# Two classes of edges in a graph network: rows of one class by one-hot products, of the other by gathers

## The chip, the cores and the metric

The kernel runs on one core of a Trainium2 chip. A core has five engines with a queue of instructions each: TensorE (PE, matrix products into PSUM; "PEld" are its weight loads), VectorE (DVE), ScalarE (ACT), GpSimd (POOL) and SyncE (SP). An engine takes its instructions in order and waits at the first whose semaphores are not reached. Transfers are issued from the queues of SP, ACT and POOL. The metric is the device time of one execution in microseconds. The PE clock that the throttle grants is told as a share of full speed.

## The reference

There are 3125 nodes with 128 features, and 53,125 edges: 25,000 random pairs in both directions and a self loop for each node, sorted by destination. Four networks follow each other, each added to its input and layer-normalised:

```python
x = LN(x + gin(x))       # 4 layers: h = x + sum of x[src] per dst; x = relu(h@W1+b1)@W2+b2
x = LN(x + relu(x@root + bias + sum_r mean over edges of type r of (x[src] @ W[r])))     # 8 types
x = LN(x + relu(sum over edges of alpha[type]*(x@w_rel[type])[src] + count*(x@update)))  # 16 types, 8 bases
x = LN(x + relu(sum over edges of gate*(x[src]@W[r] + bias[r]) + x@loop))                # 8 types
```

## The kernel before

**Dense part.** `gin_layers` (L515) builds the adjacency as a dense bf16 matrix AT of 25 blocks of 128 sources by 3125 destinations. The edges come in TE = 416 tiles of 128. For each tile, DVE writes two one-hots (L824, L826), PE multiplies them (L828, L832), and ACT copies the result into AT at a column held in a register (L835). Besides, `late(i)` (L631) does a piece of other work at the tiles of `LATE = [16, 20, 24, 28, 32, 36]`: it turns the tables of keys and source indices and writes them to DRAM (`keys`, `srcs`). After that `first_parts` splits x into three bf16 parts whose sum is the f32 value. `dense(l, j, …)` (L752) multiplies AT by the parts: 75 bf16 products per chunk of 512 destinations (L760), then the copy hT (L765) and two dense products (L768, L775); seven chunks, four layers. The first of the dense layers runs beside the loop over tiles. `checks` tests on chip that the sorted edges lie near where an even spread would put them and writes a flag; only if the flag is set does a slower program, `any_order`, run after this one.

**Relational part.** `in_order` (L924) loads the keys back, computes registers' values, and runs `relational` (L1092) three times. The edges are processed in the same 416 tiles:

- a gather (L1062): an indirect transfer, issued by POOL, of the 128 source rows into a buffer `xg` of four tiles; there are six such buffers, so gathers may run 24 tiles ahead;
- a one-hot `oh` on DVE (L1150, L1152 or L1157, by layer) of 128 edges by 16 columns x 8 types: since edges are sorted by destination, a tile is taken to touch at most W = 16 destinations;
- an f32 product `pw` on PE (L1159; the profile counts two matmuls for one f32 product), and its addition on DVE into `sums` at a column from a register (L1161). DVE loads 16 such registers at a time (`DGRP`);
- in layers 1 and 3 a product that counts the edges per type, into PSUM at an offset that PE loads to a register (L1167; one or two per tile, 728 in all per layer);
- in layer 2 coefficients per 8 tiles (L1097); in layer 3 gates from gathered columns (L1139, L1141).

When the last tile of a block of 128 destinations is done, `finish1`, `finish2` or `finish3` (L1193, L1260, L1282) multiplies the block's sums by the weights (L1183), normalises and writes the rows to the DRAM table of the next layer (`xtab`, `gtab`, or the output). ACT sets the sums back to zero (`clear`, L956). The next layer's gathers read the whole table, so they wait for the last block.

The order on each engine's queue is fixed when the kernel is built: the framework places instructions by their order in the program and adds semaphores for every dependence, buffers' reuse included.

Of the kernel before, what the change touches and what calls it, by code (L numbers as in the profile page):

```python
# [61 lines left out]
LATE = [16, 20, 24, 28, 32, 36]  # L62
# [452 lines left out]
def gin_layers(ctx: ExitStack, tc: tile.TileContext, a: dict, pre: dict, outer: ExitStack, eps, srcI, xtab):  # L515
# [13 lines left out]
    keys = dram.tile([P, 4, TE], F32, name="keys")  # L529
    srcs = dram.tile([P, TE], I32, name="srcs")  # L530

    AT = big.tile([P, NB, N + W], BF16, name="AT")
    places = keep_.tile([P, 2, TE], F32, name="places")
# [5 lines left out]
    lo, hi = pre["lo"], pre["hi"]  # L539
# [6 lines left out]
    for n, (name, pad) in enumerate((("dst", PADDST), ("src", 0), ("edge_type_8", 0), ("edge_type_16", 0))):  # L546
        eng = (nc.sync, nc.scalar)[n % 2]
        r = raw[name] = tmp.tile([QR, 4, P], I32, name="raw_" + name)
        nc.gpsimd.memset(r[96:QR], pad)
        e = a[name]  # L550
        flat = r.rearrange("q k p -> q (k p)")

        for q0, q1 in ((0, 96), (96, QR - 1)):
            eng.dma_start(flat[q0:q1, :], e[q0 * 4 * P:q1 * 4 * P].rearrange("(q p) -> q p", q=q1 - q0))
        eng.dma_start(flat[QR - 1:QR, :E - (QR - 1) * 4 * P], e[(QR - 1) * 4 * P:].rearrange("(q p) -> q p", q=1))
    early = keep_.tile([P, 1], F32, name="early")
    nc.scalar.copy(early, eps)
    make_identity(nc, ident)
    nc.gpsimd.iota(iotah, pattern=[[1, NK]], base=0, channel_multiplier=0, allow_small_or_imprecise_dtypes=True)
    nc.gpsimd.iota(iota, pattern=[[1, 2 * P]], base=0, channel_multiplier=0, allow_small_or_imprecise_dtypes=True)  # L560
# [11 lines left out]
    def fl(name, into=None):  # L572
        f[name] = into if into is not None else tmp.tile([QR, 4, P], F32, name="f_" + name)
        nc.vector.tensor_copy(f[name], raw[name])
        return f[name]
# [12 lines left out]
    sbI = tmp.tile([QR, 4, P], I32, name="sbI")  # L588
    nc.vector.tensor_scalar(sbI, raw["src"], 7, None, op0=OP.arith_shift_right)
    sb = tmp.tile([QR, 4, P], F32, name="sb")  # L590
    nc.vector.tensor_copy(sb, sbI)
    kb = tmp.tile([QR, 4, P], F32, name="kb")
    nc.vector.scalar_tensor_tensor(kb, sb, float(WK), rel, op0=OP.mult, op1=OP.add)
    mod = tmp.tile([QR, 4, P], F32, name="mod")
# [17 lines left out]
    nc.scalar.copy(hi, dst0[:, 1, :])  # L612
# [11 lines left out]
    def later(i, r):  # L624
        t = tmp.tile([P, TE], F32, name="turned", bufs=2)
        turn(t, r, nc.scalar.copy)
        nc.sync.dma_start(keys[:, i, :], t)

    turnedI = tmp.tile([P, TE], I32, name="turnedI")

    def late(i):  # L631

        if i == 0:
            turn(turnedI, f["src"], nc.vector.tensor_copy)
            nc.sync.dma_start(srcs[:, :], turnedI)
        elif i == 1:
            later(0, rel)
        elif i == 2:
            t8 = fl("edge_type_8", sb)
            later(3, t8)  # L640
        elif i == 3:
            nc.vector.scalar_tensor_tensor(mod, rel, float(R8), f["edge_type_8"], op0=OP.mult, op1=OP.add)
            later(1, mod)
        elif i == 4:
            later(2, fl("edge_type_16", kb))
        elif i == 5:
            flat = f["dst"].rearrange("q k p -> q (k p)")
            inner = f["src"].rearrange("q k p -> q (k p)")[:, :4 * P - 1]
            nc.vector.tensor_tensor(inner, flat[:, :4 * P - 1], flat[:, 1:], OP.is_gt)
            nc.vector.tensor_reduce(found, inner, AX.X, OP.add)  # L650
            tmp_ctx.close()

    def checks(own):
# [25 lines left out]
        add(1, w[:, 0:1], float(N - W), OP.is_lt)  # L679
        rows = own.tile([1, 1], F32, name="rows")  # L680
# [122 lines left out]
    with tc.tile_pool(name="g_hot", bufs=4) as hots:  # L803
        old = None
        under = []
        for t in range(TE):
# [6 lines left out]
            if t == LATE[-1]:  # L813
# [5 lines left out]
                nc.scalar.dma_start(srcI, srcs[:, :])  # L819
                sp_pool = sp_ctx.enter_context(tc.tile_pool(name="g_parts", bufs=1, side="right"))  # L820
            if t % 4 == 1 and (t - LATE[-1]) // 4 - 1 in range(NCH):
                first_parts((t - LATE[-1]) // 4 - 1)
# [22 lines left out]
    keep_ctx.close()  # L845
    ep = outer.enter_context(tc.tile_pool(name="f_edges", bufs=1))
    edges = ep.tile([P, 4, TE], F32, name="edges")
    nc.scalar.dma_start(edges, keys[:, :, :])
# [38 lines left out]
    for j in range(NCH):  # L887
        run(dense(l, j, norm))
    sp_ctx.close()
# [16 lines left out]

def low(t):
# [10 lines left out]
def first_tile(c0):  # L918

    return min(t for t in range(TE) if low(t)[1] + W > c0)  # L920
# [3 lines left out]
def in_order(ctx: ExitStack, tc: tile.TileContext, a: dict, out: bass.AP, pre: dict):  # L924
# [7 lines left out]
    ident, iota, ones, lo = (pre[k] for k in ("ident", "iota", "ones", "lo"))  # L932
# [7 lines left out]
    srcI = own.tile([P, TE], I32, name="f_srcI")  # L940
    edges = gin_layers(tc, a, pre, ctx, eps, srcI, xtab[0])
    dlr, key8, et16, et8 = (edges[:, i, :] for i in range(4))

    big = ctx.enter_context(tc.tile_pool(name="f_sums", bufs=1, side="right"))
    gat = ctx.enter_context(tc.tile_pool(name="f_gat", bufs=6, side="right"))
    ohp = ctx.enter_context(tc.tile_pool(name="f_ohp", bufs=6, side="right"))
# [6 lines left out]
    zero = const.tile([P, 1], F32, name="f_zero")  # L953
    nc.vector.memset(zero, 0.0)

    def clear(b, engine=nc.scalar.copy):  # L956
        engine(sums[:, b * P * NR:(b + 1) * P * NR], zero.to_broadcast([P, P * NR]))  # L957

    clear(0, nc.vector.tensor_copy)


    offs = const.tile([1, TE], I32, name="f_offs")
    nc.vector.tensor_scalar(offs, lo, float(NR), None, op0=OP.mult)
    seg = const.tile([1, 2, TE], I32, name="f_seg")

    def segments(t):
        c = low(t)
        return range(c[0] // SEGN, min(NSEG - 1, (c[1] + W - 1) // SEGN) + 1)

    def spots(t, i):  # L970

        if len(segments(t)) <= i:
            return 0, SEGN + W
        return tuple(min(SEGN + W, max(0, x + W - segments(t)[i] * SEGN)) for x in low(t))

    raw = const.tile([1, TE], F32, name="f_raw")
    nc.vector.memset(raw, 0.0)
    for i in range(2):
        for j in range(NSEG):
            ts = [t for t in range(TE) if len(segments(t)) > i and segments(t)[i] == j]  # L980
            if ts:
                nc.vector.tensor_scalar(raw[:, ts[0]:ts[-1] + 1], lo[:, ts[0]:ts[-1] + 1], float(W - j * SEGN), 0.0,
                                        op0=OP.add, op1=OP.max)
        nc.vector.tensor_scalar(seg[:, i, :], raw, float(SEGN + W), None, op0=OP.min)
# [10 lines left out]
    rW = load("rW", [P, R8, D], a["L1_gnn_W"].rearrange("r i o -> i r o"))  # L995
    root = load("root", [P, D], a["L1_gnn_root"])
    rbias = load("rbias", [1, D], a["L1_gnn_bias"].rearrange("(a o) -> a o", a=1))
    sel = const.tile([R8, R8, P], F32, name="f_sel")
    cnt = const.tile([R8, NP], F32, name="f_cnt")
    zeroh = const.tile([1, SEGN + 2 * W], BF16, name="f_zeroh")  # L1000
# [3 lines left out]
    def later_weights():  # L1004
# [9 lines left out]
        W2["bases"] = load("bases", [P, NBASE, D], a["L2_gnn_weight"].rearrange("b i o -> i b o"))  # L1014
        W2["gW"] = gW = load("gW", [P, R8, D], a["L3_gnn_W"].rearrange("r i o -> i r o"))
# [14 lines left out]
        V = W2["V"] = const.tile([P, R8], F32, name="f_V")  # L1030
        gconst = W2["gconst"] = const.tile([P, R8], F32, name="f_gconst")
        for r in range(R8):
            gg = wk.tile([P, D], F32, name="gg")
            nc.sync.dma_start(gg, row(a["L3_gnn_gate_weight"][r], D))
            gb = wk.tile([P, D], F32, name="gb")
            nc.sync.dma_start(gb, row(a["L3_gnn_bias_term"][r], D))
            nc.vector.tensor_tensor(gb, gb, gg, OP.mult)
            nc.vector.tensor_reduce(gconst[:, r:r + 1], gb, AX.X, OP.add)
            nc.vector.tensor_tensor(gg, gW[:, r, :], gg, OP.mult)
            nc.vector.tensor_reduce(V[:, r:r + 1], gg, AX.X, OP.add)  # L1040
        nc.vector.tensor_add(gconst, gconst, W2["ggb"])

# [8 lines left out]
        dcol = W2["dcol"] = const.tile([P, W, NBASE], F32, name="f_dcol")  # L1051
        nc.vector.tensor_copy(dcol, iota[:, :W].unsqueeze(2).to_broadcast([P, W, NBASE]))

    def values(rowap, engine, bounds):
# [3 lines left out]
            skip_runtime_bounds_check_because="the drift of every tile was checked before this path was taken")  # L1058
# [6 lines left out]
    def hots(keys_, n, name, t):  # L1065

        m = min(GRP, TE - t)
        oh = wk.tile([P, GRP, n], F32, name=name)
        nc.vector.tensor_tensor(oh[:, :m], iota[:, :n].unsqueeze(1).to_broadcast([P, m, n]),
                                keys_[:, t:t + m].unsqueeze(2).to_broadcast([P, m, n]), OP.is_equal)  # L1070
        return oh

    def rows_of(table, b):

        t = wk.tile([P, D], F32, name="xb", bufs=4)
# [16 lines left out]
    def relational(layer, table, width, finish, beside=lambda t: None):  # L1092
        counted = layer in (1, 3)
        segs, cgroups = {}, {}
        b = 0

        def coefficients(t):  # L1097

            m = min(GRP, TE - t)
            oh = hots(et16, R16, "h16", t)  # L1100
# [7 lines left out]
            c = wk.tile([P, GRP, NBASE], F32, name="coef", bufs=3)  # L1108
            nc.scalar.copy(c, pc[:, :GRP * NBASE].rearrange("p (q b) -> p q b", b=NBASE))  # L1109
            cgroups[t] = c  # L1110

        for t in range(TE):
            beside(t)
            if t % DGRP == 0:
                n = min(DGRP, TE - t)
# [227 lines left out]
```

## Time and profile before

| what | value |
|---|---|
| median of 15 runs | 2806.79 us (2798.15 to 2819.14) |
| the profiled execution | 2806.24 us |
| its span | 2804.4 us |
| mean granted PE clock | 0.697 |
| adjacency loop | about 14 to 326 us |
| dense layers 1 to 3 | 344 to 690 us |
| relational layers 1, 2, 3 | 704–1433, 1433–2081, 2081–2804 us |
| gathers: 1248 | 0.95 us of POOL each |

The profile gives for each engine its busy time, its share of the span and the number of its instructions. The span in 40 slices shows each engine's busy tenths. Register loads, branches, semaphores and the issuing of transfers are not counted as busy. A group of instructions is a line, an engine, an operation and its tiles, with the count, the busy time, the mean of one in ns, and behind the second bar the idle time of the engine just before them with what ended it: another engine's instruction, a transfer, "issue" (nothing that the profile shows) or "remote" (an unknown queue). The waits' lines give the engine, the line that waited, for what, and the total, the times and the longest in us.

### The profile page before, as it was taken

The numbers are of one execution on the slowest core, as the hardware profiler recorded it, in microseconds if no ns is written. First come the engines' busy times: TensorE is split into PE (matmuls) and PEld (weight loads), VectorE is DVE, ScalarE is ACT, GpSimd is POOL, SyncE is SP. The second block draws the span as 40 slices with busy tenths as digits, with TensorE's granted clock in tenths as the row PEclk, the third lists the DMA queues.
The fourth block names the chain that finished last, engine by engine and source line by source line (L and its number), as shares of the span: only waits on it lengthen the run. The fifth ranks groups of instructions, "written<-read, shape, count | busy, mean of one in ns | idle before, by whom it ended". The sixth has DMA issues, their size and how long they took to land.

```text
span 2804.4 us, 37365 instructions
## 1 busy us (share of the span) xinstructions
PE 1941.8 (69%) x10916; PEld 1374.2 (49%) x10916; DVE 1162.9 (41%) x4732; ACT 498.0 (18%) x1001; POOL 1195.8 (43%) x1263
## 2 busy tenths in 40 slices
PE   5798999998477667777655665556644656565666
PEld 2343444444355556656544554445533545454555
DVE  6777612123144444444433444344423334343343
ACT  5778501101200000000011222222220000000000
POOL 0000000000555555656546666666635555555552
PEclk9988899999555656565555666666665566566556
DMA  1000112021111111112111122112211221222221
GB/s 49 17 7 13 54 34 61 17 62 51 48 48 43 44 45 43 47 43 52 46 33 49 50 51 52 50 49 53 50 29 44 48 48 45 46 48 46 48 47 28
DMA packets 101231, 121.96 MB, mean 43 GB/s; under 512 B 25045, under 2 KB 80522, under 8 KB 101030
## 3 DMA queue, kind: packets, MB, share of 16 engines
q0 software_dynamic: 40000, 83.59, 12.4%
q1 hardware_dynamic: 50256, 28.48, 3.4%
q10 hardware_dynamic: 10774, 7.42, 0.9%
q8 instruction: 100, 1.64, 0.3%
q14 instruction: 101, 0.83, 0.1%
HBM read 104.55 MB, written 14.84 MB: 43 GB/s over the span
## 4 chain that ended last, share of the span: by engine, by line
PE 46%; another core or an unknown queue 20%; issue 14%; POOL 7%; DVE 7%; DMA 3%; ACT 2%; DVEq 0%; ACTq 0%; SPq 0%; POOLq 0%
PE acc L760 13%; PE pw L1159 12%; POOL xg L1062 7%; PE pm L1183 7%; PE pa L828 3%; PE pr L1204 3%; PE pc L1167 2%; DVE sums L1161 2%; PE pr L768 1%; PE pr L775 1%; DMA xg<-fx,f_srcI 1%; DMA xn<-in_x_dram 1%; PE pa L832 1%; DVE sc L1205 1%
## 5 line engine op out<-in xcount | busy, mean ns | idle before, releaser
L1062 POOL DMA_INDIRECT xg<-fx,f_srcI x832 | 795.0, 956 | 1199.9 <-DMA f_gloop<-n_L_gnn_loop_weight_dram 699.4
L1159 PE MATMUL pw<-oh,xg 128*128 128x128 f32 x2496 | 667.4, 407 | 360.8 <-issue 150.4
L1159 PEld LDWEIGHTS pw<-oh,xg 128*128 128x128 f32 x2496 | 523.2, 282 | 448.3 <-issue 189.9
L1161 DVE TENSOR_TENSOR sums<-pw,sums 128x128 f32 x1248 | 358.2, 287 | 868.9 <-remote 429.8
L1062 POOL DMA_INDIRECT xg<-gtab,f_srcI x416 | 395.3, 950 | 332.9 <-PE pw L1159 170.6
L760 PE MATMUL acc<-AT,xs 128*128 128x512 bf16 (+1 forms) x2100 | 442.4, 355 | 1.2 <-DMA xs<-xsd 1.1
L760 PEld LDWEIGHTS <-xs 128*128 128x128 bf16 x2100 | 175.8, 99 | 195.6 <-issue 20.0
L835 ACT CAST AT<-pa 128x400 f32 x416 | 213.3, 513 | 62.7 <-PE pa L832 27.7
L828 PE MATMUL pa<-ohk,ohs 128*128 128x425 bf16 x416 | 171.4, 426 | 48.6 <-ACT AT L835 25.5
L826 DVE TENSOR_SCALAR ohk<-iotah,places 128x425 bf16<-128x425 f16 x416 | 139.1, 334 | 59.7 <-PE pa L832 53.2
L957 ACT COPY sums<-f_zero 128x1024 f32<-128x1024 f32 x74 | 75.2, 1042 | 367.2 <-PE pm L1183 123.6
L1152 DVE SCALAR_TENSOR_TENSOR oh<-f_dcol,edges,coef 128x128 f32<-128x128 f32 x416 | 136.8, 343 | 0.6 <-ACT coef L1109 0.6
L1157 DVE TENSOR_SCALAR oh<-p_iota,edges,g 128x128 f32<-128x128 f32 x416 | 135.3, 353 | 0.1
L1167 PE MATMUL pc<-hw,h 128*8 128x16 f32 x1456 | 85.8, 186 | 55.8 <-issue 50.8
L1150 DVE TENSOR_SCALAR oh<-p_iota,edges 128x128 f32<-128x128 f32 x416 | 119.7, 295 | 0.0
L1204 PE MATMUL pr<-ci,f_sel 8*128 8x128 f32 x400 | 93.8, 381 | 36.4 <-DVE sc L1205 33.0
L1183 PE MATMUL pm<-f_gW,sums 128*128 128x128 f32 x400 | 100.1, 432 | 24.8 <-DVE sums L1161 18.5
L1167 PE MATMUL pc<-hw,rg 128*8 128x16 f32 x1456 | 84.0, 183 | 39.6 <-issue 20.7
L1183 PEld LDWEIGHTS pm<-f_gW,sums 128*128 128x128 f32 x400 | 97.8, 336 | 26.2 <-DVE sums L1161 19.2
L1183 PE MATMUL pm<-f_bases,sums 128*128 128x128 f32 x400 | 100.4, 434 | 9.0 <-DVE sums L1161 6.0
L1167 PEld LDWEIGHTS pc<-hw,h 128*8 128x8 f32 x1456 | 61.2, 90 | 92.4 <-issue 80.0
L828 PEld LDWEIGHTS <-ohs 128*128 128x128 bf16 x416 | 42.3, 102 | 130.4 <-DVE ohk L826 86.7
(202 smaller groups left out, 1782.9 us busy)
## 6 DMA issues: line engine op xcount, KB each, us to landing
xg<-fx,f_srcI POOLq DMA_INDIRECT x832
xsd<-sp SPq DMA_DIRECT2D x18, 384.0 KB
xg<-gtab,f_srcI POOLq DMA_INDIRECT x416
xs<-xsd SPq DMA_DIRECT2D x9, 384.0 KB
xs<-xsd ACTq DMA_DIRECT2D x9, 384.0 KB
xb<-fx SPq DMA_DIRECT2D x49, 64.0 KB
gtab<-yg SPq DMA_DIRECT2D x25, 68.0 KB
fx<-y SPq DMA_DIRECT2D x25, 64.0 KB
```

The source lines that it names most:

```text
L760: nc.tensor.matmul(acc[:, :n], xs[s // BPB][:, s % BPB, i, :], AT[:, s, c0:c1], start=s == 0 and i == 0, stop=s == NB - 1 and i == 2)
L826: nc.vector.tensor_scalar(ohk, iotah, keyb[:, t:t + 1], None, op0=OP.is_equal)
L828: nc.tensor.matmul(ps, ohs, ohk, start=True, stop=t == 0)
L835: nc.scalar.copy(AT[:, :, bass.ds(og[t % GRP], W)], ps3[:, :, :W])
L1062: nc.gpsimd.indirect_dma_start(out=dst, out_offset=None, in_=table, in_offset=bass.IndirectOffsetOnAxis(ap=idx, axis=0))
L1152: nc.vector.scalar_tensor_tensor(oh.rearrange("p (d b) -> p d b", b=NR), W2["dcol"], dlr[:, u:u + 1], cgroups[u - u % GRP][:, u % GRP, :]. ...
L1157: nc.vector.tensor_scalar(oh, iota[:, :W * NR], key8[:, u:u + 1], gate, op0=OP.is_equal, op1=OP.mult)
L1159: nc.tensor.matmul(ps, x[:, u % 4, :D], oh, start=True, stop=True)
L1161: nc.vector.tensor_tensor(w, ps, w, OP.add)
L1167: nc.tensor.matmul(segs[j][:, bass.ds(spot[i][u], W)], r, hw[:, u % GRP, :], start=False, stop=u == last_tile(min(N, (j + 1) * P)))
L1183: nc.tensor.matmul(pb, s[:, r, :], w[:, r, :], start=False, stop=r == NR - 1)
L1204: nc.tensor.matmul(pr[:, r * P:(r + 1) * P], sel[:, h + r, :], ci, start=True, stop=True)
```

## The change

The source blocks are divided. An edge whose source lies in the last KB = 6 blocks (node S0 = 2432 or above) belongs to class P, every other edge to class G. Both classes keep the order of destinations and are padded to whole tiles: NTP = 96 tiles of P with a window of WP = 48 destinations, NTG = 327 tiles of G with the window of 16.

*Sorting.* `late` no longer turns tables. It computes on DVE, over 125 partitions x 425 edges, each edge's rank in its class by a scan, and from it a slot. 425 `scatter`s, indirect transfers on POOL of 125 entries of 8 bytes (source and destination in one number, types in the other), write the entries to a DRAM table `slots`: one after each tile of the adjacency loop from tile 29 on, the last 38 after it. `first_parts` comes every 8 tiles in place of 4. After the third chunk of the last dense layer `arrange()` reads the slots back, unpacks them on DVE, and writes P's source rows to DRAM as f16.

*Relational layers.* A G tile goes as before, from a table cut to [:S0]. A P tile has no gather: `fetch` makes its 128 rows by products of one-hots of the sources with the six blocks, held in SBUF as three bf16 parts; `add_P` makes the wide product with the one-hot of destinations, adds the one column that an earlier tile may have begun, and copies the result over `sums`, which need no clearing. `upto` puts P tiles ahead of the G tiles that touch the same columns, and fetches one tile more with each G tile. `finish` of the last six blocks splits the new rows for the next layer (`keep_parts`).

Layer 1's counts are multiplied in bf16. Registers are loaded 8 at a time. The buffers for gathers are five, those for one-hots four, and the three 8-weight tables share two buffers; `gate_weights` comes before layer 2, and the checks of the new bounds, `later_keys`, at tile 100 of layer 1.

```diff
+KB = 6
+S0 = (NB - KB) * P
+NTP = 96
+NTG = 327
...
+            nc.vector.tensor_scalar(flag2, raw2["src"], float(S0), None, op0=OP.is_ge)
+            nc.vector.tensor_tensor_scan(rank, flag2, none, 0.0, OP.add, OP.add)
...
+    def scatter(c):
+        st = nc.gpsimd.indirect_dma_start(
+            out=slots[:, :], out_offset=bass.IndirectOffsetOnAxis(ap=rowI[:, c:c + 1], axis=0),
+            in_=meta[:EP2, c, :], in_offset=None)
...
+            if t > LATE[-1]:
+                scatter(t - LATE[-1] - 1)
...
+    def arrange():
+        held = meta[:, :NTT, :]
+        nc.gpsimd.dma_start(held.rearrange("p t f -> p (t f)"), slots.rearrange("(p t) f -> p (t f)", p=P))
+        nc.vector.tensor_copy(edges["dst"], held[:, :, 0])
...
     for j in range(NCH):
         run(dense(l, j, norm))
+        if j == 2:
+            arrange()
...
+    def split(x, to, tmp):
+        nc.scalar.copy(to(0), x)
+        nc.vector.tensor_tensor(tmp, x, to(0), OP.subtract)
+        nc.scalar.copy(to(1), tmp)
+        nc.vector.tensor_tensor(tmp, tmp, to(1), OP.subtract)
+        nc.vector.tensor_copy(to(2), tmp)
...
+        def fetch(v):
+            if v % 2 == 0:
+                srcb = wk.tile([P, 2 * P], F16, name="srcb", bufs=4)
+                nc.sync.dma_start(srcb, flatrow[:, v * P:(v + 2) * P].to_broadcast([P, 2 * P]))
+                ohT = hot_src[0] = wk.tile([P, KB, 2 * P], BF16, name="ohTP")
+                for k in range(KB):
+                    nc.vector.tensor_scalar(ohT[:, k, :], srcb, colid[:, k:k + 1], None, op0=OP.is_equal)
+            if v % 4 == 0:
+                fetched[v // 4] = (wk.tile([P, 4, GX], F32, name="xP"),)
+            ohT, x = hot_src[0], fetched[v // 4][0]
+            px = psum.tile([P, GX], F32, name="px", bufs=1)
+            for k in range(KB):
+                for i in range(3):
+                    nc.tensor.matmul(px[:, :width_], ohT[:, k, v % 2 * P:(v % 2 + 1) * P], parts[layer][:, k, i, :width_],
+                                     start=k == 0 and i == 0, stop=k == KB - 1 and i == 2)
+            nc.scalar.copy(x[:, v % 4, :width_], px[:, :width_])
+
+        def add_P(v):
+            x = fetched[v // 4][0]
...
+            oh = onehot(v, gate)
+            ps = psum.tile([P, BANK], F32, name="pp", bufs=1)
+            nc.tensor.matmul(ps[:, :WP * NR], x[:, v % 4, :D], oh, start=True, stop=True)
...
+            if v > 0:
+                nc.vector.tensor_tensor(ps[:, :NR], ps[:, :NR], sums3[:, bass.ds(g["lo"][q], 1), :].rearrange("p d r -> p (d r)"), OP.add)
...
+            nc.scalar.copy(sums3[:, bass.ds(g["loA"][q], WP), :], ps[:, :WP * NR].rearrange("p (d r) -> p d r", r=NR))
...
+        def upto(need, ahead):
+
+            while done[0] < min(NTP, need // 4 * 4 + 4):
+                fetch(done[0])
+                done[0] += 1
+            while done[1] <= min(need, NTP - 1):
+                add_P(done[1])
+                done[1] += 1
+            if ahead and done[0] < min(NTP, need // 4 * 4 + 8):
+                fetch(done[0])
+                done[0] += 1
...
-    relational(2, xtab[1][:, :], D, finish2)
+        keep_parts(3, b, yg[:, 0, :], GX)
+
+    new_parts(3)
+    gate_weights()
+    relational(2, xtab[1][:S0, :], D, finish2)
...
-    relational(3, gtab[:, :], GX, finish3)
+    relational(3, gtab[:S0, :], GX, finish3)
```

## The prediction

> **What bounds the kernel now.** First the page: shares of the engines, the slices, the chain.
>
> ```profile
> span 2804.4 us, 37365 instructions
> PE 1941.8 (69%) x10916; PEld 1374.2 (49%) x10916; DVE 1162.9 (41%) x4732; ACT 498.0 (18%) x1001; POOL 1195.8 (43%) x1263
> ...
> PE   5798999998477667777655665556644656565666
> ...
> POOL 0000000000555555656546666666635555555552
> PEclk9988899999555656565555666666665566566556
> ...
> PE 46%; another core or an unknown queue 20%; issue 14%; POOL 7%; DVE 7%; DMA 3%; ACT 2%; DVEq 0%; ACTq 0%; SPq 0%; POOLq 0%
> ```
>
> PE is the busiest engine, but only the first quarter (adjacency and dense layers) is dense. In the relational three quarters PE is half to two thirds busy at a granted clock of 0.5 to 0.6, and POOL, idle before, issues gathers. So the stages, by windows: 100–300 lies in the adjacency loop, 344–690 is dense layers 1 to 3, then relational layers 1, 2, 3.
>
> ```profile
> 100.00:300.00 200.00, 184.80 (x980) 81.50 (x979) 153.25 (x628) 156.98 (x307) 0.00 (x0) 0.86 0.03 9
> 344.00:690.00 346.00, 343.23 (x1826) 162.55 (x1825) 69.83 (x167) 34.61 (x60) 0.00 (x0) 1.00 0.15 45
> 704.00:1433.00 729.00, 506.42 (x3222) 412.50 (x3222) 308.01 (x1195) 57.78 (x115) 397.93 (x417) 0.60 0.17 44
> 1433.00:2081.00 648.00, 380.25 (x1605) 317.74 (x1605) 253.33 (x1063) 137.60 (x281) 398.81 (x419) 0.64 0.19 48
> 2081.00:2804.00 723.00, 429.03 (x2830) 359.61 (x2830) 274.89 (x1265) 20.73 (x74) 395.06 (x416) 0.60 0.20 45
> ```
>
> The columns are the window, its length, busy PE, PE weight loads, DVE, ACT, POOL, the clock, DMA share, GB/s. The relational layers take 2100 us: PE busy 1316, idle 784. Does the gather set the pace? Its rhythm when nothing holds it is 0.95 busy and 0.30 of issue, 1.25 us, so 416 tiles need 520 us; the layers take 729, 648 and 723. The POOL's waits in layer 1 (then layer 2), and gathers against sums (L1161) in the first part of layer 1:
>
> ```profile
> POOL xg L1062 <- PE pw L1159: 134.5, 34, 10.3
> ...
> POOL xg L1062 <- PE pw L1159: 35.7, 22, 2.6
> ...
> 703.00:1147.00 444.00, 244.69 (x256) 0.59 0.17 45
> ...
> 703.00:1147.00 444.00, 66.57 (x233) 0.59 0.17 45
> ```
>
> POOL waits 134.5 us in layer 1 for PE to free a gather buffer, and after 444 us it is 256−233 = 23 tiles ahead of 24 possible. So in layers 1 and 3 the consumers (one-hot on DVE, product on PE, sum on DVE, counts on PE) set the pace; in layer 2 the two are near level.
>
> ```profile
> L1159 PE MATMUL pw<-oh,xg 128*128 128x128 f32 x2496 | 667.4, 407 | 360.8 <-issue 150.4
> L1161 DVE TENSOR_TENSOR sums<-pw,sums 128x128 f32 x1248 | 358.2, 287 | 868.9 <-remote 429.8
> L1167 PE MATMUL pc<-hw,h 128*8 128x16 f32 x1456 | 85.8, 186 | 55.8 <-issue 50.8
> ```
>
> PE's gaps end on nothing the profile shows ("issue", "remote"): DVE, PE and ACT stand still together for 3 to 14 us while gathers go on; five-microsecond DVE stops recur about each 16 tiles, where 16 register values are loaded. The change keeps one such load per tile (416 becomes 423).
>
> **Cost, part by part.**
> *A gathered tile dropped.* PE: 667.4/1248 = 0.535 us of product, and in layers 1 and 3 (85.8+84.0)/832 = 0.204 of counts. 89 fewer tiles (416−327).
> *A one-hot tile added, 96 per layer.* Its fetch is 18 bf16 matmuls of 128 columns. The dense layers stream 512 columns in 219 ns, so 128 in 55 ns: 18 × 55 = 0.99 us at full clock. Each also has a new 128x128 weight load (99 ns in the L760 rows), so 18 × 0.10 = 1.8 if loads aren't hidden. I take 1.5, since relational PE shows loads beside matmuls at a low clock. The wide product, 384 f32 columns: three times the 128-column one is 1.5 at the relational clock; the 512-column L768 at full clock takes 1.1 for two passes, so 0.85 for 384. I take 1.2, and 0.1 for counts: 2.8 us (1.9 to 3.4), 269 us a layer (182 to 326). Less what the 89 tiles gave back (66 in layers 1 and 3, 48 in layer 2), and less 33 for layer 1's counts in one bf16 pass instead of two (327×0.204/2): +170, +221, +203, together +594. PE goes from 1316 to 1910 us at today's clock.
> *Clock.* 0.60 at 69% busy, 0.86 at 92%, 1.00 at 99%: at three quarters busy, about 0.70. 1910×0.61/0.70 = 1664.
> [...]
> *Idle.* 784 us over 1248 tiles is 0.63 a tile; 981 tiles keep 617. Fetches (96×3×1.5×0.87 = 376) depend on no gather and can fill it, but PE takes its queue in order and one fetch is issued per gathered tile: half, −188. New handoffs (product, first-column add on DVE, ACT copy into sums, which the next add reads, through one psum buffer): nearest row the bound between pw and sums, about 0.3 us exposed per tile, +86. Idle 515. Relational: 1664+515 = 2179, **+79**. Nothing filled: +267; all filled: −109.
> *DVE.* Per one-hot tile: six one-hots of 256 columns per two tiles (0.284 each, between L824's 0.247 for 128 columns and L826's 0.334 for 425) 0.85; a 384-column one-hot about 0.5 (L1157: 0.353 for 128); two small adds 0.17 each (an 8-column add is 0.166); group one-hots 0.1. That is 1.8×96 = 172, less 89×0.65 = 58: +114 on 253 to 308 a layer, beside PE. *ACT.* 0.27 + 0.47 + 0.2 per tile (copies of 128 columns take 0.266, casts of 512 take 0.617), +90 a layer on at most 138, less 75 clears of 1.04 us: beside PE. SP's row broadcasts, one per two tiles, are issued four tiles early: hidden; a landing of about 3.5 us if not. POOL falls to 327×1.25 = 409 a layer.
> *Head.* late() gets some twenty 125x425 operations on DVE; at 0.36 to 0.58 (the checks' 415-column rows), 10 us, against about 4 removed. The adjacency loop is paced by ACT and PE, DVE is 77% busy there: +6 (0 to 12). The transposes, turned copies and key transfers leave: in the 4.
> *Scatters.* 425 on POOL, idle until 700. No scatter is in the trace; as an indirect transfer of the same kind I take the gather's 1.25: 531 us from about 40 to 571. They're needed where arrange() reads them back, after chunk 2 of dense layer 3, about 633 (that layer starts at 577.5 in the timeline, a chunk takes 18.4): cost 0, dear only from 1.39 us each. The read-back waits behind them on POOL's queue, and arrange()'s unpacking waits for it at the head of DVE's, with the copies hT (L765), which the next chunks' second products need, behind it: a late scatter stops PE there. The 433 KB themselves are some 2 us at the 235 GB/s which a slice of 300–704 reaches, within a chunk. Upper bound: the longest gather, 1.65, +110. Lower bound 0.
> [...]
> *Header.* Some thirty one-row operations of 423 (0.36 to 0.58), reading the last blocks back and splitting them, while PE waits: +15 (0 to 30); part may run beside chunks 3 to 6 of the last dense layer (633 to 690).
> *Between layers.* Gathers stop 37.5 and 41.9 us there. 2→3's may now start earlier, up to 20×1.25 = 25 us of filled buffers; but layer 2's pair gathers still wait for the whole table, and the first sums need the last block's parts, a fetch of four and an add: 0 (−50 to +40). gate_weights() on SP and DVE before layer 2 is needed only by its first finished block, and later_keys() at tile 100 is some ten small DVE operations beside PE: 0, at most 10 us if DVE were the late one.
>
> **Sum.** 79+6+15 = +100 on the profiled execution's 2806.2 (span 2804.4 and 1.8 outside), 0.6 below the median: 2907.
>
> **Rivals.**
> *Faster: fetches fill PE's gaps.* Decides from a PE share of 80% (1664/(2100−21)). At 85%: 1664/0.85 = 1958, −142+21: about 2686; at the 92% of the adjacency loop 1809, 2536. For: fetches wait for no gather, and clears leave. Against: one in-order PE queue, and stops in which all engines stand. 0.37.
> *The gathers do set the pace* through something the waits don't show (the joint stops occur only while they run): 96 one-hot tiles then are nearly free and 89 gathers at 1.66, 1.45, 1.65 go: −424 on paper, 2380 as its floor; PE's 1664 keeps it above. It's counted with the faster.
> *Clock stays 0.61.* 1910 at 83% busy is 2300, +200: 3027. For: relational clock never above 0.64. 0.13.
> *Scatters late:* 3017, 0.04. *DVE becomes the bound:* 836+342 busy and as much waiting is under 2100; not likely. *The sort's checks fail and the fallback runs as well:* over twice the time; expected class sizes (11,781 of 12,288 slots) fit. 0.02.
>
> **Numbers.** Forecast, fetches half hidden: 0.44, own range 2813 (three quarters of them) to 3001 (a quarter). The range 2630 to 3080 leaves out the densest faster case and the unfilled one. A measurement here tells about 0.2% from none. Faster 0.37, same 0.03, slower 0.60.
>
> **What would show it.** Relational clock near 0.70 and PE share near 76%; fetches 1.5 us and wide products 1.2 per tile; gathers ending well ahead of PE; POOL done with scatters near 571. Wrong, if PE's share passes 80%, if the clock doesn't move, or if joint stops shrink with the number of gathers.

## The result, and the profile after

The changed kernel takes 3151.55 us (median of 9 runs, 3141.03 to 3167.51) against 2807.98 of the kernel before (47 runs): ratio 1.123, 95% interval 1.1211 to 1.1249. It is 344 us slower; the direction was forecast, the size was not, and the time lies above the range.

The page of the changed kernel, the lines that answer to those of before, and one group:

```profile
span 3157.3 us, 47896 instructions
PE 2352.3 (75%) x15205; PEld 1601.4 (51%) x15205; DVE 1499.0 (47%) x5997; ACT 638.4 (20%) x1668; POOL 1456.9 (46%) x1427
...
PE   4888600039999688888887778777887778778887
...
POOL 4777777740000343433445535555554244444442
PEclk9988855569999788778875699888897887887797
...
L926 DVE CAST e_dst<-meta 128x423 int32<-128x423 f32 x1 | 0.4, 379 | 316.2 <-DMA meta<-slots 316.2
```

The hole is in the slices 5 to 9 of the PE row, in the dense part, not in the relational one. The last line names it: the first instruction of `arrange()`'s unpacking stood 316.2 us at the head of DVE's queue, for the transfer that reads the slots back. The stages by windows (same columns as before: length, PE, weight loads, DVE, ACT, POOL, clock, DMA share, GB/s), and the timeline at the hole's end:

```profile
14.00:355.00 341.00, 261.02 (x1261) 100.92 (x1262) 268.70 (x937) 225.90 (x444) 249.75 (x207) 0.89 0.12 14
373.00:686.00 313.00, 0.15 (x6) 0.03 (x2) 1.58 (x6) 0.00 (x0) 244.22 (x208) 0.51 0.10 5
687.00:1036.00 349.00, 345.52 (x1830) 164.26 (x1830) 71.77 (x178) 35.19 (x62) 2.50 (x5) 0.99 0.14 43
1036.00:1811.00 775.00, 643.16 (x4212) 477.58 (x4212) 427.22 (x1690) 95.79 (x355) 331.79 (x347) 0.75 0.17 43
1811.00:2437.00 626.00, 500.01 (x3364) 398.29 (x3364) 352.80 (x1421) 181.31 (x457) 316.85 (x329) 0.86 0.19 47
2437.00:3157.00 720.00, 579.41 (x4411) 448.37 (x4409) 359.20 (x1673) 95.39 (x346) 293.38 (x307) 0.81 0.18 39
```

```profile
332.98 0.68 DVE L828 COPY hT<-acc 128x512 f32<-128x512 f32 x1
...
681.01 0.61 POOL L925 DMA_DIRECT2D meta<-slots  x1 [1.66 <-DMA slots<-meta,rowI]
684.38 0.38 DVE L926 CAST e_dst<-meta 128x423 int32<-128x423 f32 x1 [316.15 <-DMA meta<-slots]
...
685.78 0.68 DVE L828 COPY hT<-acc 128x512 f32<-128x512 f32 x1
686.52 2.07 PE L831 MATMUL pr<-hT,W 128*128 128x512 f32 x2 [313.38 <-DVE hT L828]
```

The order can be read line by line: scatters end, the read-back goes out, DVE unpacks, only then DVE copies the accumulator of a dense chunk (hT), and PE goes on after 313.38 us. That chunk belongs to the first dense layer, not to the last: the trace has only five copies hT ahead of the unpacking, the last of them at 332.98 us, and a dense layer has seven. From 368 us on DVE stood at the unpacking.

So the framework does not keep the text's order across independent instructions; my description of the kernel before said that it does.

The account, from the last product of L760 (L823 after), which begins at 689.1 before and at 1033.3 after: of these 344 us the stop is 313, and the adjacency loop 29 (its last cast L835, L899 after, moves from 326.0 to 355.2). Everything behind takes 2115 before and 2124 after: +9. The two profiled executions so lie 353 us apart, the medians 344.

### The profile page after: what moved, and what is told of

Its sections match the earlier page's. It is cut to its first block, busy times and chain, and to the rows that moved or that the text cites. A ratio compares the mean times of both kernels' runs of the same rounds, so it can differ in the third digit from the quotient of the medians.

```text
span 3157.3 us, 47896 instructions
## 1 busy us (share of the span) xinstructions
PE 2352.3 (75%) x15205; PEld 1601.4 (51%) x15205; DVE 1499.0 (47%) x5997; ACT 638.4 (20%) x1668; POOL 1456.9 (46%) x1427
## 5 line engine op out<-in xcount | busy, mean ns | idle before, releaser
L1262 POOL DMA_INDIRECT xg<-fx,e_src x654 | 628.9, 962 | 729.0 <-PE pw L1445 445.5
L705 POOL DMA_INDIRECT slots<-meta,rowI x425 | 507.7, 1195 | 160.1 <-issue 129.2
L1445 PEld LDWEIGHTS pw<-oh,xg 128*128 128x128 f32 x1962 | 379.4, 234 | 363.1 <-DVE sums L1447 232.6
L1378 PE MATMUL px<-f_parts,ohTP 128*128 128x128 bf16 (+1 forms) x5184 | 488.8, 242 | 44.1 <-ACT xP L1380 22.4
L1262 POOL DMA_INDIRECT xg<-gtab,e_src x327 | 312.3, 955 | 405.9 <-PE pw L1445 203.7
L823 PE MATMUL acc<-AT,xs 128*128 128x512 bf16 (+1 forms) x2100 | 444.9, 357 | 0.7 <-DMA xs<-xsd 0.7
L1378 PEld LDWEIGHTS <-ohTP 128*128 128x128 bf16 x5184 | 401.3, 110 | 76.3 <-issue 52.3
L1392 PE MATMUL pp<-ohP,xP 128*128 128x384 f32 x576 | 311.7, 630 | 23.5 <-ACT f_cntP L1403 11.3
L823 PEld LDWEIGHTS <-xs 128*128 128x128 bf16 x2100 | 176.4, 100 | 201.4 <-issue 26.9
L899 ACT CAST AT<-pa 128x400 f32 x416 | 212.7, 511 | 97.3 <-PE pa L896 55.1
L1371 DVE TENSOR_SCALAR ohTP<-srcb,f_colid 128x256 bf16<-128x256 f16 x864 | 209.8, 287 | 35.6 <-PE px L1378 16.2
L1467 PE MATMUL pm<-f_relw,sums 128*128 128x128 f32 x800 | 203.8, 425 | 16.2 <-DVE sums L1447 8.1
L1467 PEld LDWEIGHTS pm<-f_relw,sums 128*128 128x128 f32 x800 | 195.7, 335 | 27.0 <-DVE sums L1447 14.0
L926 DVE CAST e_dst<-meta 128x423 int32<-128x423 f32 x1 | 0.4, 379 | 316.2 <-DMA meta<-slots 316.2
```

Of the source, the lines that this page charges most:

```text
L705: st = nc.gpsimd.indirect_dma_start(out=slots[:, :], out_offset=bass.IndirectOffsetOnAxis(ap=rowI[:, c:c + 1], axis=0), in_=meta[:EP2, c, ...
L823: nc.tensor.matmul(acc[:, :n], xs[s // BPB][:, s % BPB, i, :], AT[:, s, c0:c1], start=s == 0 and i == 0, stop=s == NB - 1 and i == 2)
L899: nc.scalar.copy(AT[:, :, bass.ds(og[t % GRP], W)], ps3[:, :, :W])
L1262: nc.gpsimd.indirect_dma_start(out=dst, out_offset=None, in_=table, in_offset=bass.IndirectOffsetOnAxis(ap=idx, axis=0))
L1371: nc.vector.tensor_scalar(ohT[:, k, :], srcb, colid[:, k:k + 1], None, op0=OP.is_equal)
L1378: nc.tensor.matmul(px[:, :width_], ohT[:, k, v % 2 * P:(v % 2 + 1) * P], parts[layer][:, k, i, :width_], start=k == 0 and i == 0, stop=k = ...
```

## Experiments

They ran on several chips, and these are of two kinds: on two of them (and for the first result) the kernel before takes 2802 to 2830 us, on three 2350. I call them the slower and the quicker kind. Every ratio is to the kernel before on the same chip.

**Is the stop the place of the unpacking?** Its instructions are tied behind a copy hT of the last dense layer, the third chunk's (late_unpack) or, with `j == 4`, the fifth's (unpack_chunk5):

```diff
-        nc.vector.tensor_copy(hT[:, :n], acc[:, :n])
+        copied[0] = nc.vector.tensor_copy(hT[:, :n], acc[:, :n])
...
-        if j == 2:
-            arrange()
+        if j == 2:
+            with tc.issue_after(copied[0].ins):
+                arrange()
```

> The changed kernel with one thing altered: arrange()'s instructions are tied behind the copy hT of the last dense layer's third chunk on each instruction's own engine, which is where the program's text has them. Theory A (DVE's queue): the 313 us in which PE stands at 373 to 687 are a wait of the unpacking for the scatters, which stood in DVE's queue before the first copies of dense layer 0's end. Then the dense layers run through, the scatters still end near 680, and the time falls by about 308: 2843, with a PE gap of at most 20 us near 665. Theory B (the scatters' traffic itself holds the dense layers' transfers): the order on DVE is no matter, 3150.

> The changed kernel as it is, beside the kernel before on the same chip. The unpacking's wait in DVE's queue is a matter of POOL's 425 scatters and does not depend on the chip: a PE gap of about 313 us that starts near 373. Where the kernel before takes 2807 the time is 3151 as measured; where it takes 2350, it is the 2583 of the late unpacking, less its remaining stop of 44, plus 313: 2850.

> arrange()'s instructions tied behind the copy hT of the last dense layer's fifth chunk in place of the third, when the scatters (until about 682) are nearly done. Theory A: the stop of 44 us shrinks to under 10; 2543 where the kernel before takes 2350, and 2843 where it takes 2807. What is left against the kernel before lies then in the relational layers, 150 to 180 us in the first case, and in the adjacency loop, 10 to 30.

On quicker chips: the changed kernel 2869.27 (ratio 1.221, 1.2187 to 1.2232) with a PE gap of 331 us, late_unpack 2583.39 (1.0996, 1.0971 to 1.102) with one of 44.4 us, where at most 20 was expected, unpack_chunk5 2544.14 (1.0821, 1.08 to 1.0842) with one of 4.0 us there. So the place costs 325 us on that kind, and theory B falls. The gap is longer there than the 313 us of the first result because the adjacency loop ends earlier (last cast at 335.9 us) and the scatters don't (678). The same kernel as unpack_chunk5 on a slower chip:

> unpack_chunk5 again, for a chip on which the kernel before takes 2807 to 2830: 2838 if the adjacency loop ends near 355, up to 2930 if it ends near 440; the relational layers level with the kernel before. On a chip with 2350: 2545 again.

It took 2849.35, ratio 1.0157 (1.0109 to 1.0205). Its windows (loop, dense layers, three relational layers) show no hole; the clock of the dense window is 0.98, and POOL's scatters lie beside it. From the loop's last cast (351.9) to the last dense product (735.8) it takes 384 us, against 363 in the kernel before:

```profile
14.00:352.00 338.00, 261.36 (x1262) 101.74 (x1263) 263.99 (x937) 226.03 (x445) 247.34 (x205) 0.89 0.12 14
376.00:738.00 362.00, 347.08 (x1768) 162.23 (x1768) 74.03 (x180) 34.20 (x61) 246.41 (x211) 0.98 0.21 43
744.00:1517.00 773.00, 646.42 (x4213) 481.38 (x4214) 424.58 (x1673) 95.63 (x356) 328.77 (x342) 0.75 0.15 42
1517.00:2150.00 633.00, 510.21 (x3414) 408.59 (x3414) 354.25 (x1430) 184.12 (x464) 317.41 (x329) 0.85 0.17 47
2150.00:2858.00 708.00, 571.94 (x4358) 443.04 (x4357) 357.41 (x1660) 91.63 (x336) 293.52 (x307) 0.81 0.16 40
```

**What lengthens the adjacency loop?** The 425 scatters are taken out, everything else of the front part stays.

```diff
-            if t > LATE[-1]:
-                scatter(t - LATE[-1] - 1)
...
-    for c in range(TE - LATE[-1] - 1, EC2):
-        scatter(c)
```

> The changed kernel without its 425 scatters, so that every edge is padding (sums are zeroed on POOL in the header instead, the last check's result is dropped); only the adjacency loop and the dense layers are to be read. Theory A: no stop before the unpacking although it keeps its place, dense layers end near 700 us instead of 1036. Theory C (the loop's extra 29 us come from scatters that slow the 16-bit one-hots on DVE): ohk goes back from 408 to about 334 ns, ohs from 288 to 247, the adjacency loop ends near 335. Theory D (late()'s new operations lengthen the loop): it ends near 355 still, and the one-hots' means stay.

No hole, the loop's last cast at 327.4, the last dense product at 690.9. The run came on a quicker chip; there the kernel before has 328.2 and 691.2 (before_dgrp8, below), so late()'s new operations cost next to nothing (theory D falls). But with its scatters the changed kernel's last cast comes at 335.9 on that kind (after_again): the scatters cost the loop 8.5 us there, and not the 29 of the first result. DVE's two groups in the window 40 to 330, the changed kernel on the first chip, then on a quicker one, then no_scatters:

```profile
L890 DVE TENSOR_SCALAR ohk<-iotah,places 128x425 bf16<-128x425 f16 x359 | 147.8, 412 | 47.0 <-PE pa L896 34.5 <-issue 6.6 <-PE acc L823 0.8
L888 DVE TENSOR_SCALAR ohs<-iotah,places 128x128 bf16<-128x128 f16 x358 | 102.1, 285 | 0.0
```

```profile
L890 DVE TENSOR_SCALAR ohk<-iotah,places 128x425 bf16<-128x425 f16 x385 | 148.9, 387 | 36.8 <-PE pa L896 31.2
L888 DVE TENSOR_SCALAR ohs<-iotah,places 128x128 bf16<-128x128 f16 x384 | 113.6, 296 | 0.0
```

```profile
L888 DVE TENSOR_SCALAR ohk<-iotah,places 128x425 bf16<-128x425 f16 x392 | 131.2, 335 | 52.1 <-PE pa L894 46.4
L886 DVE TENSOR_SCALAR ohs<-iotah,places 128x128 bf16<-128x128 f16 x392 | 96.9, 247 | 0.0
```

While POOL scatters, the pair of 16-bit one-hots of a tile takes 697 ns on the slower chip and 683 on the quicker one, in place of 582; the 128x512 f32 subtractions of the same loop (L779, xn<-xn,xs) keep their 690 ns. So theory C holds for the one-hots, but their lengthening doesn't account for the loop: it is nearly the same on both kinds, and the loop gains 29 us on one and 8.5 on the other. Without scatters the kernel before has its last cast at 325 to 328 us on both kinds. With them it comes at 336 to 340 on quicker chips, at 352 to 355 in the first result and on one slower chip, and at 437 and 442 in the two kernels of this family that ran on the other slower chip (fetch_twice and seven_blocks, below), where the pair of one-hots takes 698 and 708 ns. By which way the scatters lengthen the loop on the slower kind is open.

A stretch of seven_blocks shows what a scatter does to a one-hot:

```profile
201.18 1.18 POOL L705 DMA_INDIRECT slots<-meta,rowI  x1 [0.30 <-issue]
201.45 0.34 DVE L892 TENSOR_SCALAR ohk<-iotah,places 128x425 bf16<-128x425 f16 x1 [0.58 <-PE pa L898]
...
201.70 0.65 DVE L890 TENSOR_SCALAR ohs<-iotah,places 128x128 bf16<-128x128 f16 x1
...
202.45 0.25 DVE L890 TENSOR_SCALAR ohs<-iotah,places 128x128 bf16<-128x128 f16 x1
202.59 0.35 PE L894 MATMUL pa<-ohk,ohs 128*128 128x425 bf16 x1
202.66 1.18 POOL L705 DMA_INDIRECT slots<-meta,rowI  x1 [0.30 <-issue]
```

The one-hot that begins 0.27 us after the scatter's start keeps its 0.34 us; the one that begins 0.52 us after it ends with the scatter, after 0.65 us; the one in the pause takes 0.25. It is so throughout: in the changed kernel's first trace, 160 of the short one-hots (ohs) begin in the first 0.45 us of a scatter, and none takes over 0.26 us; 62 are stretched, and all of these begin 0.51 to 0.85 us after a scatter's start and end within 0.02 us of its end. So the short one-hots passed in the first 0.45 us of a scatter and were held from about 0.5 us after its start to its end; by what is not shown.

**Do the joint stops come from the register batches?** The kernel before, with `DGRP = 8` in place of 16:

> The kernel before with registers loaded on DVE 8 at a time in place of 16, as the changed kernel does. If the joint stops of 3 to 14 us in the relational layers are the waits for a batch of 16 loads, smaller batches let the sums go on sooner and PE's idle time (784 us) falls by 50 or more: 2750. If a load instruction of 16 costs 1.1 us, as the trace has it, and the stops have another cause, the time stays within 20 us of 2807.

Ratio 1.0019 (1.001 to 1.0029). The chip was of the quicker kind, on which PE has few such stops (its gaps over 2.5 us in the three relational layers sum to 64 us, for 458 in the first profile), so this run doesn't decide it. Two other things do: the load takes 1.10 us for 16 registers and 0.60 for 8, and half_pool_c, just below, keeps the batches of 16 on a slower chip and loses nearly all the stops. The "five-microsecond stops where 16 values are loaded" were not those loads.

**Do they come from the gathers?** The kernel before, with every second gather replaced by a plain transfer from SP's queue, as many bytes:

```diff
-            gather(xg[:, t % 4, :width], table, srcI[:, t:t + 1])
+            if t % 2 == 0:
+                gather(xg[:, t % 4, :width], table, srcI[:, t:t + 1])
+            else:
+                nc.sync.dma_start(xg[:, t % 4, :width], table[t % 24 * P:(t % 24 + 1) * P, :])
```

> The kernel before with every second gather replaced by a plain transfer of 128 consecutive rows from SP's queue: as many bytes, half of POOL's gathers; odd tiles so use the wrong rows. If the consumers set the pace, layers 1 and 3 keep their 740 and 726 us within 20 and only layer 2 gains, down to some 600. If the issuing of gathers is what stops all engines together, PE's gaps over 2.5 us (210 us in layer 3) halve, and layers 1 and 3 fall by 70 to 100 each.

> half of the gathers replaced by plain transfers (odd tiles use wrong rows), for a chip with 2807 to 2830: theory S (the joint stops come with POOL's indirect transfers) 2150 to 2350; theory T (they have nothing to do with POOL) 2600 or more. On a chip with 2350: 2015 again.

On a quicker chip 2023.13; on a slower one 2166.86 in place of 2802.32, ratio 0.7736 (0.7696 to 0.7776). The difference between the two kinds of chip falls from 451 us (2802.32−2351.42) to 152 (2166.86−2014.63, half_pool_b), and PE's gaps over 2.5 us in layer 3 sum to 10 us, for 219 in the first profile: theory S. PE's longest sums of waits in layer 3 of the kernel before on a slower chip (690 us of it), and the same places in half_pool_c (450 us of it; its lines are numbered 3 higher); the columns are place, total us, times, longest:

```profile
PE pm L1290 <- ACT xT L1088: 56.0, 16, 5.6
PE pm L1291 <- ACT ci L1286: 55.6, 9, 7.8
PE pw L1159 <- DVE oh L1157: 55.2, 26, 18.7
```

```profile
PE pm L1293 <- ACT xT L1088: 23.1, 16, 2.0
PE pm L1294 <- ACT ci L1289: 20.5, 13, 2.2
...
PE pw L1162 <- DVE oh L1160: 8.4, 12, 4.1
```

The same places wait, and the mean wait at each is half as long or shorter. So on the slower kind of chip POOL's indirect transfers lengthen the handoffs of the other engines, though POOL itself waits for PE. By which way they do it is not shown (the plain transfers also read consecutive rows in place of scattered ones, so the issue and the traffic changed together), nor what makes the chips differ.

The first of these two views is of the kernel before itself, run once for a profile on an experiment's chip:

> The kernel before, for a profile on the chip on which the experiments run. Theory: where it takes 2350 us it lacks the joint stops of the first profile (PE's gaps over 2.5 us in layer 3: 210 us there); then DVE waits for the transfers of gathers, POOL issues them every 1.25 us without a stop, and each relational layer takes 520 us and a restart of 25 to 40.

It met the slower kind (2827.33), so the expectation for the quicker kind went untested there. For that kind before_dgrp8 stands in: its relational layers, from first gather to first gather, take 551, 553 and 546 us, near the 520 of 416 gathers at 1.25 and a restart.

**Does the fetch cost time?** Only the first of three bf16 parts is multiplied, 6 products in place of 18 (`for i in range(1)`), and the other way every product twice (`range(6)`, part `i % 3`).

> unpack_chunk5 with only the first of the three bf16 parts in fetch: 6 products per one-hot tile in place of 18; two thirds of the fetched rows' precision work is left out. 12 x 288 products of some 85 ns are 294 us of PE. Theory P (PE is the bound in the changed relational layers, 88% busy): 230 to 290 us less than unpack_chunk5. Theory Q (my forecast: half of the fetch lies in PE's gaps): about 150 less. Theory G (gathers or handoffs set the pace): under 50.

> two thirds of the fetch's products left out, for a chip with 2807 to 2830: theory K 0 to 80 us more than unpack_chunk5_c, theory P 230 less. On a chip with 2350: 65 more again.

On the quicker chip 2610.86 against 2544.14 of unpack_chunk5: two thirds of the fetch less, and 67 us *more*; on another of that kind 2610.09 against 2549.30. On the slower chip 2830.73 against 2849.35: 19 us less, for 3456 products of 0.096 us (497.8 over 5184 in unpack_chunk5_c), 332 us of PE. The relational windows of fetch_one_part_c, to be held against the last three of unpack_chunk5_c above:

```profile
739.00:1515.00 776.00, 647.92 (x3055) 454.96 (x3056) 420.33 (x1670) 94.87 (x357) 333.87 (x342) 0.62 0.15 41
1515.00:2149.00 634.00, 496.41 (x2260) 367.17 (x2260) 357.83 (x1432) 183.06 (x463) 320.27 (x329) 0.73 0.17 46
2149.00:2825.00 676.00, 538.91 (x3212) 386.72 (x3211) 359.26 (x1660) 92.45 (x336) 294.54 (x307) 0.71 0.17 41
```

A quarter to a third of PE's instructions is gone and PE's busy time is nearly as before: the clock fell from 0.75, 0.85, 0.81 to 0.62, 0.73, 0.71, and what was left got longer (the wide product from 623 to 712 ns; in layer 2, PE's 2262 instructions beside the 1152 products left out took 400 us by that account, 510.21 − 1152 × 0.096, and the 2260 that remain take 496). Theory P falls. Theory K has the clock, the sign and the size on quicker chips; on the slower one it said 0 to 80 us more, and 19 less was measured.

> unpack_chunk5 with every fetch product made twice into the same accumulator, so that fetched rows come out doubled: 5184 products more. fetch_one_part took two thirds of the fetch away and got 67 us slower at a clock of 0.80 in place of 0.86. Theory K (the fetch lies in PE's gaps and keeps the clock up; the pace is set by the lockstep of products, sums and copies): the clock rises towards 0.95 and the time grows by less than 150 us. Theory P (PE is the bound): 5184 x 0.085 = 440 us more, 2985.

3255.00, ratio 1.1509 (1.147 to 1.1548), on a slower chip on which unpack_chunk5 did not run. Its three relational layers take 2428 us (829 to 3257) against 2114 in unpack_chunk5_c on another chip of that kind: some 310 more for 5184 products, at a clock of 0.79, 0.88 and 0.86. Neither theory has it: K said under 150 and a clock towards 0.95, P 440. The gaps seem to hold about the fetch that there is, not twice as much; what sets the pace of the changed relational layers is not shown.

**Is six the right size?** Five and seven source blocks (KB, NTP, NTG, WP of 5, 80, 344, 56 and 7, 112, 309, 40):

> unpack_chunk5 with five source blocks by one-hots in place of six: KB 5, 80 one-hot tiles with a window of 56, 344 gathered tiles. PE per layer: 80x15 fetch products in place of 96x18 (-528 x 0.085 = -45), 16 wide products fewer (-16) which are a sixth wider (+8), 17 gathered tiles more (+13). Theory P: 40 a layer, 120 us less than unpack_chunk5. Theory G: 17 gathers more at 1.25 each, 64 us more.

> unpack_chunk5 with seven source blocks by one-hots: KB 7, 112 one-hot tiles with a window of 40, 309 gathered tiles (and three buffers for rows and one-hots in place of four, for room). Five blocks took 128 us more than six. Theory K: fewer gathered tiles with their handoffs, a denser PE, a higher clock: 40 to 130 us less than unpack_chunk5. Theory P: 112x21-96x18 = 624 fetch products more per layer, 53 us, and 16 wide products, against 18 gathered tiles: 40 a layer, 120 more in all.

> seven_blocks again, against unpack_chunk5 on the same chip. Theory K: 40 to 130 us less than it. Theory P: 120 us more.

Five: 2671.74 on the chip of the 2544.14, 128 us more, against both theories' numbers. Seven: 2543.88 on a quicker chip, where unpack_chunk5 took 2549.30: the same; on a slower one 3040.62 (1.0732, 1.0666 to 1.0798), of which the adjacency loop, with its last cast at 442.4, has some 115 us. These sizes also change the number of tiles, the windows and, for seven, the buffers, so that no single price follows from them.

No size or place of the change that was run beats the kernel before; with the whole fetch unpack_chunk5 is the nearest, 1.016 on a slower chip and 1.08 on quicker ones.

## Why the prediction was wrong

**The step that failed** is "They're needed where arrange() reads them back, after chunk 2 of dense layer 3, about 633 … cost 0". The mechanism stood in the next sentence (the unpacking at the head of DVE's queue, the copies hT behind it, a late scatter stops PE there), but its place was taken from the program's text. In the built queue it stood three dense layers earlier, at 368 us, where the scatters had 311 us to go: PE stood for 313 us. Tied to where the text has it, the stop falls to 44 us on a quicker chip, and two chunks later it is gone on both kinds (unpack_chunk5).

**The price of a scatter** was taken as the gather's 1.25 us, with 1.65 as upper bound and 1.39 as the point from which it matters. It is 1.195 + 0.30 = 1.50, and the scatters end near 680, not 571. By itself that is the 44 us of late_unpack on a quicker chip. At 1.25 in the built place the wait would still have been some 200 us, by my estimate (571−368). The rival "scatters late" had the cause, 0.04 of the chance, and the price of the wrong place.

**Head:** late() at +6 was too much (next to nothing). The loop's +29 comes with the scatters, which the forecast lacked: I had counted POOL's queue as idle and its use as free.

**Relational layers and header,** forecast +94 and measured +9. By the windows the layers took 2121 us for 2100, +21 where I had +79, and the header 12 us less where I had 15 more. PE's busy time held, 1723 for 1664; its terms only in part. A wide product, forecast at 1.2, took 311.7/288 = 1.08, and a fetch, forecast at 1.5 or 1.31 at the higher clock, took 488.8/288 = 1.70. The clock came to 0.75, 0.86, 0.81 in place of 0.70, at a PE share of 81% for 76%. I had read the clock from the busy share, though my own rows gave 0.60 at 69% and 0.64 at 59%. Idle was mis-sized: 398 in place of 515. "Half of the fetch hidden" was too little for a slower chip; taking two thirds of it away saves 19 us there, of 332. "Joint stops shrink with the number of gathers", which I named as what would make me wrong, is what happened on this kind of chip, and further than the number: gathers fell from 1248 to 981, and PE's gaps over 2.5 us in layer 3 from 219 us to 24. Which part of the change did that was not tried.

**The reading behind it:** "256−233 = 23 tiles ahead", hence the consumers set the pace. The count was right and the conclusion wasn't: half_pool_c shows that on this kind of chip the gathers slow the consumers (2802.32 us with all of them, 2166.86 with half). Nor did PE's gaps end on nothing that the profile shows: in the view of layer 3 above, the longest sums wait for ACT and DVE. The rival "the gathers do set the pace through something the waits don't show" had its premise right; its 424 us weren't gained, and what took their place isn't shown, since two thirds of the fetch's products gave back only 19.

With the stop removed the same kernel is at 2849, inside the forecast's own range of 2813 to 3001, and that is partly luck. In the profile of unpack_chunk5_c the loop takes 26 us more than in the first profile of the kernel before and the dense layers 21, for which I had 6 and 0; what lies behind takes 8 more, for which I had 94.

**On quicker chips** the kernel before has few of the stops. From the last dense product to the end it takes 1664 us there (before_dgrp8), and the change 1836 (unpack_chunk5_b): a loss. It isn't simply PE's added products, since leaving two thirds of the fetch out makes it 61 to 67 us longer.

## What to carry to other kernels

A wait that a change adds belongs to a place in a queue, and that place is the built one: before pricing an added wait, look where the scheduler puts its instruction, and tie it if the place matters. An engine that waits for others can still be what slows them (POOL waited 134.5 us for PE in layer 1, and with half of its gathers the kernel took 0.7736 of its time on a slower chip); halving its instructions is the test, a count of how far ahead it is isn't. Taking work out of a busy engine may save next to nothing (332 us out of PE saved 19 on a slower chip, and on quicker ones the time grew by 61 to 67); only a run without it shows its price. And where chips differ, a pair of runs from two chips shows no cause: the loop's 29 us looked explained until the same kernel was read on the other kind.

## What the runs showed of the hardware

- The same kernel takes 2350 us on three chips and 2802 to 2830 on others, with equal durations of single instructions off PE (sums 287 ns, gathers 0.95 us on both); the difference is in the waits (DVE stands idle for 869 us ahead of its sums in the first profile, for 327 in before_dgrp8), and two thirds of it, 451 us down to 152, go when half of POOL's gathers are replaced by plain transfers.
- In the changed kernel's first trace 62 of VectorE's 16-bit one-hots of 0.25 us, begun 0.51 to 0.85 us after the start of a scatter on POOL, were stretched to the scatter's end (up to 0.67 us); the 160 begun in a scatter's first 0.45 us were not. The mean of the 128x512 f32 subtractions (L779, xn<-xn,xs) in the same loop is 690 ns with scatters and 691 without (no_scatters).
- An indirect transfer that scatters 125 entries of 8 bytes takes POOL 1.195 us, one that gathers 128 rows of 512 bytes 0.95: fewer bytes, and more of POOL's time.
- With a third of its products gone, PE's busy time stayed nearly as it was: 510 and 496 us in layer 2 (unpack_chunk5_c, fetch_one_part_c), at a clock of 0.85 and 0.73.
